# A four-layer decoder: VectorE and ScalarE in the order of the written table through the local transformer, the latent attention and the cross attention

## The chip, the core and the metric

The kernel runs on one core of a Trainium2 chip. Five engines work side by side: TensorE (PE, its weight loads shown as PEld), VectorE (DVE), ScalarE (ACT), GpSimd (POOL), and SyncE (SP), which issues transfers. Each engine takes its own instructions in a fixed order and waits at each for what it needs. The metric is the device time of one execution in microseconds; a profiled execution gives the trace that the views below come from.

## The reference

The program is a decoder of four layers on 32 sequences of 64 tokens with 128 features (2048 tokens). Each of its twelve stages is added to its input and put through a layernorm, `x = layernorm(x + stage(x))`:

- layer 0: self-attention with 16 heads of 8, a gated cross attention, and a *local transformer*;
- layer 1: a latent attention (16 heads of 64), a cross attention (16 heads of 8), and a mixture of 8 experts;
- layer 2: attention, cross attention and a second mixture of experts;
- layer 3: attention, cross attention and an fp8 linear layer.

The change touches mostly the local transformer, the latent attention and the first of layer 1's cross attentions. The local transformer is itself two layers deep. One of its layers, with 8 heads of 64 in which a query looks at its own sequence causally, is

```
qkv = shift(x) @ wqkv                 # half of the features from the token before
q, k = l2norm(q), l2norm(k); q, k = rotary(q, k)
x = x + softmax(q k^T) v @ wo
h = layernorm(shift(x)) * g + b
a, g = split(h @ w1 + b1)
x = x + (a * gelu(g)) @ w2 + b2
```

The latent attention projects queries directly and keys and values through a latent vector of 64, rotates queries and keys, and has no feed-forward part.

## The kernel before

All tensors stay on chip between stages. Tokens are kept in 4 blocks of 512 (NBLK), each as 4 tiles of 128 tokens (TPB), on one side with tokens on partitions (`xt`), on the other transposed (`xT`).

**The table.** Work is written as small functions that are put into a table under a step and a place in that step, `sp.at(step, place, f)`; `Steps.run` calls them in sorted order. TensorE always takes its instructions in that order. VectorE and ScalarE do so only in steps that lie in one of the ranges of `sp.fixed`, which are (95, 129) and (136, 197) before the change. Elsewhere a planner orders them, and it orders GpSimd and SyncE everywhere, from its own estimates of durations and with the table's order as priority. All waits between engines follow from the data.

**Steps.** The first attention begins at step 0, the gated cross attention at 14, the local transformer at 23 (16 tiles for each of its two layers), the latent attention at 55 (16 tiles), the cross attention `l1x` at 71 (16 score steps), then routing and experts, and from 96 on layer 2.

**One tile.** `tiles64` spreads a tile i over five steps. With "lag" counted from the step of i: `start` (lag 0, place 1) projects queries, keys and values into PSUM (`qkps`, `v`); in the local transformer ScalarE squares `qkps` (`sq`, line 1125) and copies `v`, VectorE sums the squares per head (`rn`, 1129), GpSimd raises them to the power -1/2 (1130 and the next line). `rope` (lag 0, 2.3) makes three VectorE products with the cosine and sine tables (`turn`), which GpSimd adds and multiplies by `rn`. `rotate` (lag 2, place 0) transposes the result on TensorE (`ropeT`, 969) and ScalarE copies it (`qk`, 970). `score` (lag 2, place 2) multiplies queries with keys into `s`; VectorE takes the maxima (`mx`, 988) and subtracts them (`p`), and ScalarE takes the exponential at once (992). `normal` (lag 2, 2.6) sums `p`, takes the reciprocal and multiplies: on VectorE with 8 heads (the local transformer, `nh == 4`), with the product on GpSimd with 16. `probs` (lag 3, place 4) transposes `p` (`ptps`, copied as `pT`, 1011), `values` (lag 3, place 6) multiplies with the values (`o`, copied as `oT`, 1027), `out` (lag 4, place 5) applies `wo` and, every second tile, adds to the residual on VectorE (`x` in the local transformer, `z` in the latent attention).

So step n holds rotate(n-2), start(n), score(n-2), rope(n), normal(n-2), probs(n-3), out(n-4), values(n-3), n being the tile's number.

**The feed-forward part**, once per block of four tiles, is placed around these. With n the block's first step: `shifted` (n-1, place 7) makes the shifted input `hT` with two ScalarE copies and one GpSimd memset (1103 to 1106); `normed` (n+7, 7) shifts the attention's result with a matmul (`shps`), copies it to `xs` on ScalarE, takes its statistics on VectorE and the inverse deviation on GpSimd (`rstd`), and scales on VectorE (1173); `turn_h` (n+8, 7) transposes `xs` (`hnT`); `hidden` (n+9, 7) multiplies with w1 in three chunks (`gps`, `aps`), gelu on ScalarE, product on VectorE (`ge`); `second` (n+10, 3) adds the bias row and residual on GpSimd (`resid`), multiplies with w2, adds on VectorE (`acc`), and in the second layer computes and applies the stage's layernorm (`norm`: statistics on VectorE, `rstd` on GpSimd, `nb` on VectorE, four scalings `x` on ScalarE). The latent attention calls `norm` in the same way from `done`, at a block's last tile, and `turn_x` transposes the result two steps later.

**PSUM.** Two buffers "S" of 1024 columns are shared by `qkps` and `s`, four buffers "G" of 512 columns by everything else; a matmul waits until its buffer's last reader is done.

**attn8 and routing.** In `l1x` the exponential stands at place 0.01 of its score's step; in attentions that are `held` or `ahead` at 6.5. With `split`, the last block is finished in two halves: `turn` and `normal_rest` of the second half stand at places 6.5 and 6.4 of step base+17 in the cross attentions `l1x` and `l2x` (the last one, `l3x`, has places of its own). Routing (`routed`) works in five pieces of 4, 4, 4, 2 and 2 tiles of tokens: logits, compare, choose, chosen, rows, then per tile `places` and `scatter`, one indirect transfer in GpSimd's queue each. In step `ready`+9 stand the third piece (places 1.1 to 4.4), the fourth (4 to 6.3) and the fifth (7 to 7.5); after them come the expert tables with the loads of the sorted rows through SyncE's queue (`tables`, in layer 2 `loads`).

Of the kernel before, what the change touches and what calls it, by code (L numbers as in the profile page):

```python
# [16 lines left out]
AF = mybir.ActivationFunctionType  # L17
# [264 lines left out]
class Decoder:  # L282
# [392 lines left out]
    def attn8(self, sp, base, name, src=None, rope=None, scale=1.0, row=None, mask=(None, None), has_out=True, split=False, number=False, turned=None, ahead=None, held=False):  # L675
# [142 lines left out]
        for blk in range(NBLK):  # L818
            for i in range(3):
                n = base + 4 * blk - 4  # L820
                at = (n + 1 + (i + 1) // 2, 4 + i % 2 / 2) if held and blk else (n + i, 4)
                sp.at(*at, lambda blk=blk, i=i: prepare(blk, i))
            sp.at(base + 4 * blk + (1 if split and not has_out else 2), 5.5, lambda blk=blk: resid(blk))
            if halved(blk):
                sp.at(*((base + 16, 6.5) if turned is None else (base + 16, 5.8)), lambda blk=blk: turn(blk, (0, 2)))
                sp.at(*((base + 17, 6.5) if turned is None else (base + 17, 2.1)), lambda blk=blk: turn(blk, (2, 2)))
                sp.at(*((base + 16, 6.4) if turned is None else (base + 16, 5.3)), lambda: normal_rest(0))
                sp.at(*((base + 17, 6.4) if turned is None else (base + 17, 2)), lambda: normal_rest(1))
            else:
                at = (base + 4 * blk + 8, 6) if has_out or blk < NBLK - 2 else (base + 16, 4.1)  # L830
                sp.at(*at, lambda blk=blk: turn(blk, (0, TPB)))
        if split and not has_out:
            sp.at(base + 15, 0.4, last_rest)
        for n in range(4 * NBLK):
            sp.at(base + n, 0, lambda n=n: score(n))
            sp.at(base + n, 6.5 if held or ahead else 0.01, lambda n=n: exps(n))
            end = split and n == 4 * NBLK - 1
            sp.at(*((base + n + 1, 4) if end else (base + n + 2, 2)), lambda n=n: turn_p(n))
            sp.at(*((base + n + 1, 6.1 if has_out else 5.6) if end else (base + n + 2, 5)), lambda n=n: values(n))
# [132 lines left out]
    def scores64(self, qT, kT, nh):  # L972
# [17 lines left out]
        self.tt(pr.rearrange("p n u k -> p u n k"), s4, bc(mx, 3, S), ALU.subtract)  # L990
        p3 = pr.rearrange("p n u k -> p (n u) k")
        nc.scalar.activation(p3, p3, AF.Exp)
        return p3

# [36 lines left out]
    def tiles64(self, sp, first, n, project, twist, turn, nh, wo, done):  # L1031
# [15 lines left out]
        def score(i):  # L1047
            (q, k), v = st[i]
            st[i] = (self.scores64(q, k, nh), v)

        def normal(i):
            self.normal64(st[i][0], nh)
# [20 lines left out]
        for i in range(n):  # L1073
            for lag, place, f in (
                (2, 0, rotate), (0, 1, start), (2, 2, score), (0, 2.3, rope), (2, 2.6, normal), (3, 4, probs), (4, 5, out),
                (3, 6, values),
            ):
                sp.at(first + i + lag, place, lambda f=f, i=i: f(i))


    def local_transformer(self, sp, base, names):

        nc = self.nc
        cur, tabs = {}, []

# [26 lines left out]
        def project(i):  # L1112
# [13 lines left out]
            v = self.q2([P, 2, 4, 64], "v64")  # L1126
            nc.scalar.copy(v, vp)
            rn = self.sb([P, 16], "rn", 3)
            nc.vector.tensor_reduce(rn, sq, AX.X, ALU.add)  # L1129
            nc.gpsimd.tensor_scalar(rn, rn, 1e-24, None, ALU.max)  # L1130
            self.tt(rn, rn, self.nhalf[:, 0:16], ALU.pow, nc.gpsimd)
            return (ps, rn), (v[:, 0], v[:, 1])

        def twist(i, t):
            ps, rn = t
            tab = tabs[i // 16]
            full = lambda a: a.unsqueeze(2).to_broadcast([P, 2, 8, 64])
            t1 = self.rope64(ps, full(tab[:, :, 0, :]), full(tab[:, :, 1, :]))
            self.tt(t1, t1, bc(rn, 2, 64), ALU.mult, nc.gpsimd)
            return t1  # L1140
# [18 lines left out]
        def normed(l, blk):  # L1159
# [8 lines left out]
            for t in range(TPB):  # L1168
                nc.vector.bn_stats(st[:, t, :], xs[:, t, :])
                nc.vector.bn_aggr(mv[:, t, :], st[:, t, :])  # L1170
            r = self.rstd(mv[:, :, 1], TPB)
            for t in range(TPB):
# [15 lines left out]
        def hidden(l, blk):  # L1188
# [10 lines left out]
            ff[l, blk] = hs  # L1199

        def second(l, blk):
            w, hs = self.w[names[l]], ff.pop((l, blk))
            x1 = x1s.pop((l, blk))
            xb = self.residual(x1, self.rows[f"l0f_b2{l}"])
            if l:
                self.tt(xb, xb, cur[0, blk], ALU.add, nc.gpsimd)
# [12 lines left out]
        self.tiles64(sp, base, 32, project, twist, turn, 4, lambda i: self.w[names[i // 16]]["wo"], done)  # L1219
        for l in range(2):  # L1220
            for blk in range(NBLK):
                n = base + 16 * l + 4 * blk
                for lag, place, f in ((-1, 7, shifted), (7, 7, normed), (8, 7, turn_h), (9, 7, hidden), (10, 3, second)):
                    sp.at(n + lag, place, lambda f=f, l=l, blk=blk: f(l, blk))
                if l:
                    sp.at(n + 12, 3, lambda blk=blk: self.turn_x(blk))


    def latent_attn(self, sp, base, name):

        nc = self.nc
        tab = self.c["r1"].rearrange("p (c s d) -> p c s d", c=2, d=64)
        lats, zs = {}, {}

# [43 lines left out]
        def done(i, y):  # L1278
# [100 lines left out]
    def routed(self, sp, st, ready, wr, br, base, rows, dst, bound, gated):  # L1379
# [29 lines left out]
        def scatter(t0, t):  # L1409
# [29 lines left out]
    def sorted_experts(self, sp, name, ready, fetched, tiles, back):  # L1439
# [136 lines left out]
        sp.at(*fetched, fetch)  # L1576
        sp.at(ready + 9, 8.1, tables)
        for j, at in enumerate(tiles):
# [12 lines left out]
    def capacity_experts(self, sp, name, ready, fetched, tiles, back):  # L1591
# [275 lines left out]
def decoder_kernel(ctx: ExitStack, tc: tile.TileContext, ins, at, out):  # L1867
# [76 lines left out]
```

## Time and profile before

| | |
|---|---|
| runs, median of 3 | 1419.74 us (1419.65 to 1423.8) |
| the profiled execution | 1420.89 us, its span 1419.1 us |
| mean granted TensorE clock | 0.912 |
| busy, PE / DVE / ACT / POOL | 1214.1 / 934.2 / 687.9 / 742.1 us |
| from step 29's first projection to the last score of `l1x` | 212.24 to 865.73 us of the span |
| the last score of `l1x` to the first sorted rows on TensorE | 865.73 to 900.28 us, PE busy 18.35 us |

A row of the timeline has the start, the length, the engine, line and operation, what it writes and reads, and in brackets the engine's idle time before it with what ended that. In a view by windows each row has the window, its length, the busy time of PE, PEld, DVE, ACT and POOL with counts, the granted clock (1 is full), the DMA share and GB/s. A view of waits lists who waited for whom: total, times, longest. Many operations share a helper's line (343 for matmuls, 346 for elementwise operations of two tensors), so they are told apart by tile names.

### The profile page before, as it was taken

The page shows a single profiled execution, that of the slowest core. Times are in us where ns is not written, and L with a number is a line of the kernel's source. Part 1 is how long each engine was busy: PE and PEld are TensorE (multiplying, and loading weights), DVE is VectorE, ACT ScalarE, POOL GpSimd, SP SyncE. Part 2 cuts the span into 40 slices and gives each one's busy share as a digit, 9 for nine tenths or more (in the row PEclk, how much of TensorE's full clock was granted, in tenths as well). Part 3 has the DMA queues.
Part 4 walks back from the last instruction along what each step waited for, and adds up shares of the span by engine and source line. Part 5 has one row for each costly group of instructions (what it writes and reads, how often), then busy time and mean ns, then how long its engine had stood idle before and what let it go on. Part 6 is the DMA issues. An engine that isn't in the chain of part 4 may idle for free.

```text
span 1419.1 us, 37013 instructions
## 1 busy us (share of the span) xinstructions
PE 1214.1 (86%) x16009; PEld 881.2 (62%) x16009; DVE 934.2 (66%) x1856; ACT 687.9 (48%) x1172; POOL 742.1 (52%) x618
## 2 busy tenths in 40 slices
PE   7998888899888978998898998697999948889991
PEld 4775455566555555666567776594678747567771
DVE  6754667778876766756575575554668743756797
ACT  2453445555555444544455553363556524344552
POOL 3533688767876664544464244352355443336553
PEclk9999889999999989999999997697999968879995
DMA  6001010080010000010001100220001101000001
GB/s 239 3 2 26 1 46 1 28 271 2 1 55 1 1 1 1 2 68 2 2 2 35 36 2 28 70 78 23 9 3 48 37 8 29 9 9 3 2 2 30
DMA packets 33715, 43.16 MB, mean 30 GB/s; under 512 B 5946, under 2 KB 27121, under 8 KB 33168
## 3 DMA queue, kind: packets, MB, share of 16 engines
q1 hardware_dynamic: 31536, 38.20, 8.4%
q8 instruction: 126, 2.06, 0.6%
q0 software_dynamic: 2016, 2.60, 0.6%
q14 instruction: 37, 0.30, 0.1%
HBM read 26.63 MB, written 15.56 MB: 30 GB/s over the span
## 4 chain that ended last, share of the span: by engine, by line
PE 49%; DVE 20%; POOL 14%; ACT 8%; issue 6%; DMA 2%; POOLq 0%; SPq 0%; DVEq 0%; ACTq 0%
PE s L343 10%; PE o L343 9%; DVE turn L346 5%; POOL turn L346 5%; PE qkps L343 5%; PE ptps L669 5%; PE proj L343 4%; PE y L343 3%; PE ropeT L969 3%; DVE p L346 2%; ACT pT L671 2%; DVE rn L1129 2%; POOL token_y L1362 2%; POOL rn L346 2%; POOL rstd L346 2%
## 5 line engine op out<-in xcount | busy, mean ns | idle before, releaser
L346 POOL TENSOR_TENSOR turn<-turn,turn 128x1024 f32<-128x1024 f32 x64 | 150.8, 2364 | 97.0 <-DVE turn L346 96.5
L656 DVE TENSOR_REDUCE mx<-s 128x16 f32<-128x1024 f32 x96 | 117.3, 1222 | 115.4 <-PE s L343 108.6
L346 DVE TENSOR_TENSOR p<-s,mx 128x1024 f32<-128x1024 f32 (+1 forms) x144 | 158.9, 1103 | 6.0
L671 ACT COPY pT<-ptps 128x512 f32<-128x512 f32 x192 | 103.9, 588 | 81.0 <-PE ptps L669 79.1
L726 ACT ACTIVATE p<-p 128x1024 f32<-128x1024 f32 x96 | 101.3, 1056 | 49.9 <-DVE p L346 49.7
L343 PE MATMUL s<-kx,q 32*64 32x128 f32 x3072 | 111.3, 283 | 6.0 <-DVE q L346 2.7
L346 DVE TENSOR_TENSOR turn<-qkps,w_const 128x512 f32<-128x512 f32 (+1 forms) x96 | 75.9, 858 | 58.6 <-PE qkps L343 58.6
L440 POOL TENSOR_SCALAR rstd<-bnmv 128x4 f32<-128x4 f32 (+1 forms) x60 | 16.6, 276 | 181.9 <-DVE bnmv L489 157.0
L343 PEld LDWEIGHTS s<-kx,q 32*64 32x64 f32 x3072 | 87.1, 137 | 37.9 <-issue 30.9
L669 PE MATMUL ptps<-w_const,p 128*128 128x128 f32 x768 | 109.4, 288 | 0.7 <-ACT p L726 0.5
L669 PEld LDWEIGHTS ptps<-w_const,p 128*128 128x128 f32 x768 | 90.4, 148 | 10.1 <-issue 8.5
L346 POOL TENSOR_TENSOR rn<-rn,nhalf 128x16 f32<-128x16 f32 x32 | 93.8, 2932 | 2.7
L343 PEld LDWEIGHTS o<-v,pT 128*64 128x64 f32 x2176 | 73.5, 141 | 33.8 <-ACT pT L671 16.5
L594 POOL TENSOR_TENSOR kx<-k,w_const 128x1024 f32<-128x1024 f32 x31 | 59.2, 1929 | 65.2 <-ACT k L603 31.1
L969 PE MATMUL ropeT<-w_const,turn 128*128 128x128 f32 x512 | 71.1, 286 | 24.7 <-ACT oT L1027 11.0
L343 PE MATMUL o<-v,pT 128*64 128x18 f32 x2176 | 82.2, 215 | 6.4 <-ACT pT L671 4.7
L969 PEld LDWEIGHTS ropeT<-w_const,turn 128*128 128x128 f32 x512 | 59.5, 146 | 36.3 <-ACT oT L1027 10.2
L346 DVE TENSOR_TENSOR turn<-qkps,xtab 128x512 f32<-128x512 f32 (+1 forms) x96 | 81.9, 857 | 0.0
L1129 DVE TENSOR_REDUCE rn<-sq 128x16 f32<-128x1024 f32 x32 | 39.0, 1217 | 62.6 <-ACT sq L1125 62.6
L343 PE MATMUL o<-pT,v 64*64 64x64 f32 x2048 | 72.3, 224 | 8.9 <-ACT pT L1011 8.9
L509 POOL TENSOR_SCALAR x<-z,bnmv,rstd 128x128 f32<-128x128 f32 x98 | 78.1, 810 | 2.6
L343 PE MATMUL qkps<-wbig,hT 128*128 128x512 f32 x128 | 71.0, 683 | 9.7 <-POOL hT L1105 8.8
(345 smaller groups left out, 2811.3 us busy)
## 6 DMA issues: line engine op xcount, KB each, us to landing
sorted_x<-zero SPq DMA_DIRECT2D x9, 990.0 KB
wbig<-in_l1f_w_dram SPq DMA_DIRECT2D x4, 1156.0 KB
wbig<-in_l2f_w_dram SPq DMA_DIRECT2D x16, 256.0 KB
wbig<-in_l0f_dram SPq DMA_DIRECT2D x2, 1561.0 KB
z<-token_y SPq DMA_DIRECT2D x8, 256.0 KB
wbig<-in_l1a_dram SPq DMA_DIRECT2D x1, 1856.0 KB
xsorted<-sorted_x SPq DMA_DIRECT2D x23, 66.0 KB
xT<-in_xT_dram SPq DMA_DIRECT2D x4, 256.0 KB
```

Of the source, the lines that this page charges most:

```text
L343: self.nc.tensor.matmul(out, lhsT=lhsT, rhs=rhs, start=start, stop=stop)
L346: (eng or self.nc.vector).tensor_tensor(out=out, in0=a, in1=b, op=op)
L440: nc.gpsimd.tensor_scalar(r[:, :n], var, EPS, None, ALU.add)
L509: eng.tensor_scalar(x[:, t0 + t, :], z[:, t0 + t, :], mv[:, t, 0:1], r[:, t : t + 1], ALU.subtract, ALU.mult)
L594: self.wide = eng.tensor_tensor(out=kx, in0=bc(kT, 1, 2), in1=bc(head[:, 2 * i : 2 * i + 2], 2, TB), op=ALU.mult).ins
L656: nc.vector.tensor_reduce(mx, s3, AX.X, ALU.max)
L669: self.nc.tensor.transpose(ps[:, j, :], flat[:, c : c + P], self.ident)
L671: self.nc.scalar.copy(o, ps)
L726: nc.scalar.activation(prs[n], prs[n], AF.Exp)
L969: self.nc.tensor.transpose(pt[:, j * P : (j + 1) * P], f[:, j * P : (j + 1) * P], self.ident)
L1129: nc.vector.tensor_reduce(rn, sq, AX.X, ALU.add)
L1362: i = self.nc.gpsimd.indirect_dma_start(dst, bass.IndirectOffsetOnAxis(at, 0), src, None, bounds_check=bound, oob_is_err=False).ins
```

## The change

VectorE and ScalarE are put in the table's order in the steps 29 to 88 as well (`sp.fixed.append((29, n + 18))`, where n is 71), and the range that ended before step 129 now ends before 130. In these steps places are changed:

- `tiles64`: `exps` becomes a function of its own at lag 2, place 6.5; `normal` moves to lag 3, place 0.5 (8 heads) or lag 2, place 6.6 (16 heads); `rope` moves from 2.3 to 1.5. In the transformer the sums of squares and their power (`rn`) move from `project` behind the three products in `twist`.
- Feed-forward: `shifted` to (n-1, 3.5); `normed` to (n+8, 1.7), with its scaling split off as `centred` at (n+9, 0.6); `turn_h` to (n+9, 3.5); the sum of residual, bias row and (second layer) the layer's input split off from `second` as `biased` at (n+7, 7), three steps ahead, on GpSimd.
- The closing layernorms of transformer and latent attention are split: statistics where they were, the scaling as `ended` at place 6.6 of the same step.
- `attn8`: the exponential at 6.5 everywhere but in the first attention; the second half's `normal_rest` and `turn` at 4.06 and 4.07 in `l1x` and `l2x`.
- Routing: the fourth piece from 6 to 6.3 up to 4.6 to 4.9, the fifth piece's logits from 7 to 4.5; `tables` and `loads` to the next step.

```diff
-                sp.at(*((base + 17, 6.5) if turned is None else (base + 17, 2.1)), lambda blk=blk: turn(blk, (2, 2)))
+                sp.at(*((base + 17, 4.07) if turned is None else (base + 17, 2.1)), lambda blk=blk: turn(blk, (2, 2)))
...
-                sp.at(*((base + 17, 6.4) if turned is None else (base + 17, 2)), lambda: normal_rest(1))
+                sp.at(*((base + 17, 4.06) if turned is None else (base + 17, 2)), lambda: normal_rest(1))
...
-            sp.at(base + n, 6.5 if held or ahead else 0.01, lambda n=n: exps(n))
+            sp.at(base + n, 6.5 if base else 0.01, lambda n=n: exps(n))
...
-        nc.scalar.activation(p3, p3, AF.Exp)
-        return p3
+        return pr.rearrange("p n u k -> p (n u) k")
...
+        def exps(i):
+            nc = self.nc
+            nc.scalar.activation(st[i][0], st[i][0], AF.Exp)
...
-                (2, 0, rotate), (0, 1, start), (2, 2, score), (0, 2.3, rope), (2, 2.6, normal), (3, 4, probs), (4, 5, out),
-                (3, 6, values),
+                (2, 0, rotate), ((3, 0.5) if nh == 4 else (2, 6.6)) + (normal,), (0, 1, start), (0, 1.5, rope), (2, 2, score), (3, 4, probs), (4, 5, out),
+                (3, 6, values), (2, 6.5, exps),
...
-            rn = self.sb([P, 16], "rn", 3)
-            nc.vector.tensor_reduce(rn, sq, AX.X, ALU.add)
-            nc.gpsimd.tensor_scalar(rn, rn, 1e-24, None, ALU.max)
-            self.tt(rn, rn, self.nhalf[:, 0:16], ALU.pow, nc.gpsimd)
-            return (ps, rn), (v[:, 0], v[:, 1])
+            return (ps, sq), (v[:, 0], v[:, 1])
...
+            t1 = self.rope64(ps, full(tab[:, :, 0, :]), full(tab[:, :, 1, :]))
+            rn = self.sb([P, 16], "rn", 3)
+            nc.vector.tensor_reduce(rn, sq, AX.X, ALU.add)
             nc.gpsimd.tensor_scalar(rn, rn, 1e-24, None, ALU.max)
             self.tt(rn, rn, self.nhalf[:, 0:16], ALU.pow, nc.gpsimd)
             self.tt(t1, t1, bc(rn, 2, 64), ALU.mult, nc.gpsimd)
...
+        def biased(l, blk):
+            xb = biases[blk] = self.residual(x1s[l, blk], self.rows[f"l0f_b2{l}"])
+            if l:
+                self.tt(xb, xb, cur[0, blk], ALU.add, nc.gpsimd)
...
-                self.norm(blk, x2, pool=False)
+                ends[blk] = x2, self.moments(blk, x2)
+        def ended(blk):
+            x2, moments = ends.pop(blk)
+            self.normed(blk, x2, moments, False)
...
-                for lag, place, f in ((-1, 7, shifted), (7, 7, normed), (8, 7, turn_h), (9, 7, hidden), (10, 3, second)):
+                for lag, place, f in (
+                    (-1, 3.5, shifted), (7, 7, biased), (8, 1.7, normed), (9, 0.6, centred), (9, 3.5, turn_h), (9, 7, hidden), (10, 3, second),
+                ):
...
+                    sp.at(n + 10, 6.6, lambda blk=blk: ended(blk))
...
-                self.norm(blk, zs.pop(blk), pool=False)
+                ends[blk] = self.moments(blk, zs[blk])
...
+            sp.at(base + 4 * blk + 7, 6.6, lambda blk=blk: ended(blk))
...
-            (12, 2, [(n + 9, 4)], (n + 9, 4.05), (n + 9, 6), (n + 9, 6.1), (n + 9, 6.2), [(n + 9, 6.3)] * 2),
-            (14, 2, [(n + 9, 7)], (n + 9, 7.1), (n + 9, 7.2), (n + 9, 7.3), (n + 9, 7.4), [(n + 9, 7.5)] * 2),
+            (12, 2, [(n + 9, 4)], (n + 9, 4.05), (n + 9, 4.6), (n + 9, 4.7), (n + 9, 4.8), [(n + 9, 4.9)] * 2),
+            (14, 2, [(n + 9, 4.5)], (n + 9, 4.51), (n + 9, 7.2), (n + 9, 7.3), (n + 9, 7.4), [(n + 9, 7.5)] * 2),
...
-        sp.at(ready + 9, 8.1, tables)
+        sp.at(ready + 10, 0, tables)
...
-        sp.at(ready + 9, 8.1, loads)
+        sp.at(ready + 10, 0, loads)
...
+    sp.fixed.append((29, n + 18))
...
-    sp.fixed.append((n - 1, n + 33))
+    sp.fixed.append((n - 1, n + 34))
```

More of the change, by code (lines that the diff above doesn't have):

```diff
@@ L990, in scores64 @@
         self.tt(pr.rearrange("p n u k -> p u n k"), s4, bc(mx, 3, S), ALU.subtract)
-        p3 = pr.rearrange("p n u k -> p (n u) k")
-        nc.scalar.activation(p3, p3, AF.Exp)
-        return p3
+        return pr.rearrange("p n u k -> p (n u) k")
     def normal64(self, p3, nh):
@@ L1083, in local_transformer @@
         nc = self.nc
-        cur, tabs = {}, []
+        cur, tabs, ends, biases = {}, [], {}, {}
         def tables():
@@ L1127, in project, with twist @@
             nc.scalar.copy(v, vp)
+            return (ps, sq), (v[:, 0], v[:, 1])
+        def twist(i, t):
+            ps, sq = t
+            tab = tabs[i // 16]
+            full = lambda a: a.unsqueeze(2).to_broadcast([P, 2, 8, 64])
+            t1 = self.rope64(ps, full(tab[:, :, 0, :]), full(tab[:, :, 1, :]))
             rn = self.sb([P, 16], "rn", 3)
@@ L1131, in project @@
             self.tt(rn, rn, self.nhalf[:, 0:16], ALU.pow, nc.gpsimd)
-            return (ps, rn), (v[:, 0], v[:, 1])
[L1134 to L1138, printed above, removed]
             self.tt(t1, t1, bc(rn, 2, 64), ALU.mult, nc.gpsimd)
@@ L1169, in normed, with centred @@
                 nc.vector.bn_stats(st[:, t, :], xs[:, t, :])
+            for t in range(TPB):
                 nc.vector.bn_aggr(mv[:, t, :], st[:, t, :])
-            r = self.rstd(mv[:, :, 1], TPB)
+            ff[l, blk] = xs, mv, self.rstd(mv[:, :, 1], TPB)
+        def centred(l, blk):
+            xs, mv, r = ff[l, blk]
             for t in range(TPB):
@@ L1199, in hidden @@
             ff[l, blk] = hs
+        def biased(l, blk):
+            xb = biases[blk] = self.residual(x1s[l, blk], self.rows[f"l0f_b2{l}"])
+            if l:
+                self.tt(xb, xb, cur[0, blk], ALU.add, nc.gpsimd)
         def second(l, blk):
             w, hs = self.w[names[l]], ff.pop((l, blk))
[L1203 to L1206, printed above, removed]
+            x1s.pop((l, blk))
+            xb = biases.pop(blk)
             y = self.ps8("G", "y2")
@@ L1232, in latent_attn @@
         tab = self.c["r1"].rearrange("p (c s d) -> p c s d", c=2, d=64)
-        lats, zs = {}, {}
+        lats, zs, ends = {}, {}, {}
         def latent(blk):
@@ L1284, in done, with ended @@
             if t == TPB - 1:
-                self.norm(blk, zs.pop(blk), pool=False)
+                ends[blk] = self.moments(blk, zs[blk])
+        def ended(blk):
+            self.normed(blk, zs.pop(blk), ends.pop(blk), False)
         self.tiles64(sp, base, 16, project, lambda i, t: t, turn, 8, lambda i: self.w[name]["wo"], done)
```

## The prediction

> **What bounds the kernel now.** First the page's head: span, busy shares, chain that ended last.
>
> ```profile
> span 1419.1 us, 37013 instructions
> PE 1214.1 (86%) x16009; PEld 881.2 (62%) x16009; DVE 934.2 (66%) x1856; ACT 687.9 (48%) x1172; POOL 742.1 (52%) x618
> ...
> PE 49%; DVE 20%; POOL 14%; ACT 8%; issue 6%; DMA 2%; POOLq 0%; SPq 0%; DVEq 0%; ACTq 0%
> ```
>
> TensorE is busy 86% of the time and half the chain, so a gain can only come out of TensorE's idle time (and of a lower clock after it). So I cut the changed stretch into blocks of four steps of the local transformer (window, length, busy PE, PEld, DVE, ACT, POOL, granted clock):
>
> ```profile
> 348.54:392.63 44.09, 39.22 (x441) 26.09 (x439) 34.60 (x55) 24.41 (x39) 33.34 (x20) 1.00 0.01 1
> 392.63:436.72 44.09, 39.22 (x440) 26.08 (x439) 34.61 (x55) 24.42 (x39) 33.35 (x20) 1.00 0.13 45
> 436.72:489.46 52.74, 43.02 (x444) 28.42 (x443) 36.88 (x64) 26.31 (x44) 36.01 (x23) 0.94 0.01 1
> 489.46:545.57 56.11, 46.73 (x459) 31.46 (x457) 37.48 (x68) 25.87 (x45) 29.81 (x18) 0.91 0.01 1
> ```
>
> A quiet block idles 4.87 us; the two in which the second layer's closing layernorm falls idle 9.7 and 9.4 us and run slower. From step 29 (212.24 us) to the last scores of the cross attention (865.73) these are TensorE's waits, the largest first:
>
> ```profile
> PE s L343 <- ACT qk L970: 11.3, 3, 4.0
> PE ropeT L969 <- ACT oT L1027: 11.0, 7, 2.5
> PE s L343 <- DVE turn L346: 10.1, 16, 2.5
> PE shps L343 <- DVE x L346: 9.4, 6, 1.8
> PE ropeT L969 <- ACT lat L1239: 7.7, 2, 3.9
> PE o L343 <- ACT pT L1011: 7.0, 10, 2.2
> ```
>
> With the smaller ones some 70 us: the ceiling of a gain, and every wait is for VectorE or ScalarE. How the present order makes them is read in the timeline (start, length, engine, operation, idle before). A quiet step, then the layernorm's:
>
> ```profile
> 361.84 1.22 DVE L1129 TENSOR_REDUCE rn<-sq 128x16 f32<-128x1024 f32 x1 [1.82 <-ACT sq L1125]
> 362.98 1.21 DVE L346 TENSOR_TENSOR turn<-qkps,xtab 128x1024 f32<-128x1024 f32 x1
> 364.11 0.68 DVE L988 TENSOR_REDUCE mx<-s 128x8 f32<-128x512 f32 x1
> 364.71 0.68 DVE L346 TENSOR_TENSOR turn<-qkps,xtab 128x512 f32<-128x512 f32 x1
> 366.50 0.41 DVE L346 TENSOR_TENSOR x<-y,x 128x256 f32<-128x256 f32 x1
> 366.66 2.37 POOL L346 TENSOR_TENSOR turn<-turn,turn 128x1024 f32<-128x1024 f32 x1 [0.24 <-ACT p L992]
> 366.97 0.70 PE L343 MATMUL shps<-x,w_const 128*128 128x256 f32 x2 [1.70 <-DVE x L346]
> ```
> ```profile
> 452.76 0.16 DVE L522 SCALAR_TENSOR_TENSOR nb<-bnmv,rstd 128x4 f32<-128x4 f32 x1 [1.25 <-POOL rstd L346]
> 452.96 1.65 ACT L515 ACTIVATE x<-acc,nb,rstd 128x128 f32<-128x128 f32 x4 [6.09 <-DVE nb L522]
> 454.51 1.04 ACT L970 COPY qk<-ropeT 128x512 f32<-128x512 f32 x2
> 455.61 0.69 PE L343 MATMUL s<-qk,qk 64*64 64x64 f32 x32 [4.00 <-ACT qk L970]
> ```
>
> VectorE waits 1.82 us for ScalarE's squares while the rotation's products, whose input is there, stand behind; the shift matmul stands in TensorE's queue 1.70 us before its input; and the layernorm's four scalings sit in ScalarE's queue, waiting for VectorE (6.09 us idle), ahead of the copies that the scores need.
>
> **The change, part by part.** No arithmetic is added or removed: the same instructions, in an order written out for VectorE and ScalarE, with TensorE's order edited.
>
> *Shift matmul* from (7,7) to (8,1.7): it comes after the next step's projections, about 3 us of matmuls later (qkps 1.9, v 1.1), so its 1.70 us wait goes once per block. Its statistics now stand on VectorE between the row sums of squares and the scores' maxima: four bn_stats and four aggregates, 1.4 us (369.50 to 370.8 before).
>
> *hT* from (-1,7) to (-1,3.5): the waits of qkps for it (0.47 in quiet blocks, 3.06 and 1.97 at two places) go; its two copies (0.6 each) now stand ahead of pT in ScalarE, which delays "o" some 0.5 once per block.
>
> *Products before row sums of squares* (rn): VectorE starts at qkps' end. The power on GpSimd (2.93) then runs after its add (2.36), not before: from the row sums' end 0.25 + 2.93 + 2.2, ready about 10.5 us after qkps' end, as now (360.7 to 371.3); TensorE takes it two steps on, at least 15 us. Hidden by that margin; without it 1 to 2 us a tile.
>
> *Softmax sums a step later, exponentials at 6.5.* Here the change adds a wait. The exponential stands behind oT, the last copy of a step; behind it in ScalarE stand the layernorm's scalings and the next step's qk copies, for which the scores wait. VectorE then has one closed loop per step: sum, reciprocal, product 0.65 + 0.2 + 1.65 (the product's mean of 29 is 1650 ns), rotation 2.4, row sums 1.2, maxima 0.6, subtraction 0.65, then out to ScalarE and back 0.9 (exponential 0.63 and two hand-overs): 8.25 us. TensorE needs 7.4 in a bare step (qkps to the end of o 358.87 to 365.27, ropeT 1.0). The step with the statistics needs 9.65 against 7.9. So VectorE falls about 2.6 us behind in two steps and catches up under hidden (5.8 us of matmuls) and second (2.8). Laid out over four steps, TensorE waits for the centred rows at hnT about 1.7, for qk 0.5, for pT 0.5, and 1.1 in crumbs (ropeT behind a late GpSimd, gps behind the gelu): 3.8 in place of 4.87.
>
> *Table loads.* Each block keeps two switches between exponential and gelu, but one now lies between oT and the exponential at the end of second's step, on VectorE's loop. The row: the load at 343.85 took 1.28 and the gelu began at 345.14, nothing in between. The Trainium skill (ScalarE: Activation LUTs, What ACT_TABLE_LOAD costs) counts a drain of about 1.38 with it, 2.66 in all; by that eight blocks would lose up to 11 us more. I take the row, and leave the 11 to the range.
>
> *biased* three steps ahead: 1.1 (layer two 2.4) of GpSimd leaves the wait of acc (0.93 on VectorE); it can delay one GpSimd product.
>
> *Closing layernorm a step behind* (ended at 6.6). In the transformer nb no longer blocks: statistics after second, 1.3 us of GpSimd, then nb at the step's end. The scalings (1.65) now come after the exponential, and delay qk: the scores wait about 1.9 instead of 4.0, and the waits that followed (1.80, 1.97) fall away. In the latent attention the same order gives reduction and nb about 3.5 us after o ends, scalings to 5.3, lat copy to 5.8, while TensorE stands from 2.5: 3.3 instead of 3.8.
>
> *Clock.* After the 4.00 us gap the block's matmuls ran slower (y 1.92 against 1.06): busy 43.02 against 39.22. The skill (TensorE: Matmul & The Clock Gate, Part 1) puts the drop at an idle window of about 3.4 us. By that the latent's 3.3 would keep the clock, worth some 2 us each; but here the 3.06 us gap at 281.52 was already followed by qkps at 3.00 for 1.88. I take the row: the clock returns in the transformer's two blocks (1.9), not in the latent.
>
> *Cross attention and routing.* TensorE waits there only a few us (93.67 busy of 101.48), so 0. In the tail the last half block's transpose and logits come earlier (logits of tiles 14 and 15 about 2 us here, 4 us after the second cross attention), but the end is set by GpSimd's queue: eight scatters about 1.27 us apart from 886.36 to 896.75, started by the third piece, whose place is kept. Moving the fourth piece's scatters ahead and the tables to a later step lets nothing start earlier: -1 for both tails, between -3 and +3.
>
> **Sum.** Quiet blocks from 212 to 437 (five): 1.1 x 5 plus half of the two odd hT waits, -8. The two layernorm blocks: each would save 2 + 1.8 + 2 in waits and about 3 in clock less what new waits take, 5 of 7 to 9 taken, -10. Transformer's last two blocks, which overlap the latent, and the latent's three: -4. Tails -1. Together -23 on the profiled execution's 1420.89 (span 1419.1): 1398. The runs' median is 1.15 lower: **1397**.
>
> **Rivals.**
> - *A, as summed* (0.52): 1397, own range 1383 to 1411.
> - *B, larger gain* (0.16): VectorE's loop hides fully under hidden and second, and quiet blocks fall to busy time plus 1 (40.2): 3.9 x 5 + 9 x 2 + 7: about 45, 1375. For it: VectorE is busy 34.6 of 44; against: the loop of 8.25 over 7.4.
> - *C, new waits for old* (0.10): the block stays at 44; the layernorm's gain is spent on the latent. 1419, within 0.3%.
> - *D, slower* (0.22): the strict loop. VectorE's 34.6 a block plus the return trip decides when a trip costs over 2.3 us (34.6 + 4 x 2.3 + 0.3 = 44.1): with GpSimd late or the exponential behind a table load it may be 3, 46.9 a block; over 7.5 blocks +21: 1440. For it: every wait here is a hand-over, and now nothing passes a late one.
>
> **How the numbers follow.** 0.3% (4 us) is what a measurement can tell. Faster: A and B, 0.68; same: C, 0.10; slower: D, 0.22. Range: from B's 1375 less 3 to most of D's lower half, 1372 to 1434, which leaves out about 2 in 10.
>
> **What would show it.** Right: the wait of shps for x gone; a quiet block near 43 us with a wait of hnT for xs; the 4.00 us waits of s for qk at about 2; the granted clock of the layernorm blocks near 1; the tails within 1 us. Wrong: p L992 (exponential) waits that grow past 2 us, ropeT waiting for GpSimd's turn, or ScalarE's qk late in every step.

## The result and the profile after

The changed kernel takes 1465.87 us (median of 4 runs, 1462.41 to 1472.56) against 1420.57 for the kernel before in the same comparison: 1.032 times the time, 95% interval 1.029 to 1.035. The forecast was 1397. The head of the page of the changed kernel:

```profile
span 1464.2 us, 37029 instructions
PE 1226.4 (84%) x16009; PEld 884.4 (60%) x16009; DVE 906.4 (62%) x1856; ACT 684.5 (47%) x1172; POOL 734.5 (50%) x618
...
PE 53%; DVE 16%; POOL 15%; ACT 8%; issue 4%; DMA 2%; SPq 1%; POOLq 0%; DVEq 0%; ACTq 0%
```

VectorE, ScalarE and GpSimd all have less to do than before (DVE 906.4 for 934.2), and TensorE, with the same 16009 matmuls, is busy 12.3 us longer: its clock was lower (mean 0.902 for 0.912). So the 45.1 us that the span grew are 32.8 us more idle time of TensorE and 12.3 us of slower matmuls. By windows, cut at the same steps as before (window, length, busy PE, PEld, DVE, ACT, POOL, granted clock, DMA):

```profile
373.21:425.21 52.00, 42.30 (x440) 27.03 (x439) 31.28 (x55) 24.33 (x39) 32.12 (x20) 0.93 0.00 1
...
477.22:533.99 56.77, 44.46 (x445) 29.07 (x443) 32.27 (x64) 26.37 (x44) 34.70 (x23) 0.91 0.00 1
533.99:585.94 51.95, 44.62 (x459) 29.45 (x458) 35.74 (x70) 25.35 (x45) 29.36 (x18) 0.93 0.01 1
```

A quiet block of four steps grew from 44.09 to 52.00 us: idle from 4.87 to 9.70, busy from 39.22 to 42.30 at a clock of 0.93 instead of 1.00, although VectorE is busy 31.3 us in it and was busy 34.6. Where the 45.1 us lie, against the terms of the sum:

| stretch | predicted | measured |
|---|---|---|
| up to step 29 | 0 | +4.0 |
| five quiet blocks | -8 | +36.5 |
| the two blocks with the closing layernorm | -10 | -0.1 (+4.0, -4.2) |
| rest of the transformer, latent attention | -4 | +3.7 |
| `l1x` to its last score | 0 | +1.2 |
| its tail; everything behind it | -1 | +3.4; -3.5 |

TensorE's waits in that stretch (who, for whom, total, times, longest), with four of the largest:

```profile
PE qkps L343 <- POOL hT L1107: 26.2, 6, 4.6
PE hnT L1189 <- DVE xs L1179: 16.5, 6, 3.4
PE ropeT L969 <- ACT qk L970: 12.1, 8, 3.6
PE s L343 <- ACT qk L970: 10.9, 3, 4.2
```

The first was 5.9 us before, the second was not in that list, and each comes once in six blocks. The first names GpSimd, in an instruction that clears 64 by 8 numbers. In the timeline (start, length, engine, operation, idle before):

```profile
389.40 2.36 POOL L346 TENSOR_TENSOR turn<-turn,turn 128x1024 f32<-128x1024 f32 x1 [3.09 <-DVE turn L346]
391.72 0.26 POOL L1139 TENSOR_SCALAR rn<-rn 128x16 f32<-128x16 f32 x1
392.06 2.93 POOL L346 TENSOR_TENSOR rn<-rn,nhalf 128x16 f32<-128x16 f32 x1
395.07 1.90 POOL L346 TENSOR_TENSOR turn<-turn,rn 128x1024 f32<-128x1024 f32 x1
397.03 0.11 POOL L1107 MEMSET hT<- 64x8 f32 x1
397.19 3.78 PE L343 MATMUL qkps<-wbig,hT 128*128 128x512 f32 x4 [4.44 <-POOL hT L1107]
```

Sum, maximum, power, product: GpSimd runs the four without a break, and the memset of 0.11 us behind them. It reads nothing. TensorE stands for 4.44 us, and then takes 3.78 us for projections that take 1.88 at full clock. The next step's chain has the inverse deviation of the layernorm in the same place:

```profile
406.36 0.36 DVE L1173 BATCH_NORM_AGGREGATE bnmv<-bnst 128x2 f32<-128x6 f32 x4
410.29 1.90 POOL L346 TENSOR_TENSOR turn<-turn,rn 128x1024 f32<-128x1024 f32 x1
412.27 0.23 POOL L440 TENSOR_SCALAR rstd<-bnmv 128x4 f32<-128x4 f32 x1
412.59 1.04 POOL L346 TENSOR_TENSOR rstd<-rstd,nhalf 128x4 f32<-128x4 f32 x1
413.66 1.12 DVE L1179 TENSOR_SCALAR xs<-xs,bnmv,rstd 128x128 f32<-128x128 f32 x4 [3.29 <-POOL rstd L346]
414.15 1.01 PE L1189 MATMUL hnT<-w_const,xs 128*128 128x128 f32 x4 [2.63 <-DVE xs L1179]
```

The statistics are done at 406.72 (`bnmv`, the first row); `rstd` starts 5.55 us later, when the product is off GpSimd. VectorE, in the table's order, waits for it and lets nothing pass. The closing layernorm, which the change was to take out of the way of the scores, shows the same chain (its statistics were done at 486.85), and the scores wait 4.22 us where it was 4.00:

```profile
490.42 0.23 POOL L440 TENSOR_SCALAR rstd<-bnmv 128x4 f32<-128x4 f32 x1
490.73 1.04 POOL L346 TENSOR_TENSOR rstd<-rstd,nhalf 128x4 f32<-128x4 f32 x1
491.80 0.16 DVE L522 SCALAR_TENSOR_TENSOR nb<-bnmv,rstd 128x4 f32<-128x4 f32 x1 [4.96 <-POOL rstd L346]
492.00 1.65 ACT L515 ACTIVATE x<-acc,nb,rstd 128x128 f32<-128x128 f32 x4 [3.08 <-DVE nb L522]
493.56 1.04 ACT L970 COPY qk<-ropeT 128x512 f32<-128x512 f32 x2
494.65 1.10 PE L343 MATMUL s<-qk,qk 64*64 64x64 f32 x32 [4.22 <-ACT qk L970]
```

### The profile page after: what moved, and what is told of

The parts are those of the page before. It is cut to its first block, busy times and chain, and to the rows that moved or that the text cites. A ratio compares the mean times of both kernels' runs of the same rounds, so it can differ in the third digit from the quotient of the medians.

```text
span 1464.2 us, 37029 instructions
## 1 busy us (share of the span) xinstructions
PE 1226.4 (84%) x16009; PEld 884.4 (60%) x16009; DVE 906.4 (62%) x1856; ACT 684.5 (47%) x1172; POOL 734.5 (50%) x618
## 4 chain that ended last, share of the span: by engine, by line
PE 53%; DVE 16%; POOL 15%; ACT 8%; issue 4%; DMA 2%; SPq 1%; POOLq 0%; DVEq 0%; ACTq 0%
PE s L343 11%; PE o L343 9%; POOL turn L346 6%; PE y L343 5%; DVE turn L346 5%; PE qkps L343 5%; PE ptps L669 5%; PE proj L343 5%; POOL rn L346 4%; ACT pT L671 2%; PE ropeT L969 2%; PE ptps L1007 2%; PE aps L343 1%; PE gps L343 1%; DVE p L346 1%
## 5 line engine op out<-in xcount | busy, mean ns | idle before, releaser
L346 DVE TENSOR_TENSOR turn<-qkps,xtab 128x512 f32<-128x512 f32 (+1 forms) x96 | 77.5, 861 | 79.6 <-ACT sq L1127 79.6
L343 PE MATMUL qkps<-wbig,hT 128*128 128x512 f32 x128 | 77.6, 738 | 29.7 <-POOL hT L1107 29.7
L996 DVE TENSOR_REDUCE rec<-p 128x8 f32<-128x512 f32 (+1 forms) x48 | 41.4, 862 | 77.6 <-ACT p L1051 77.6
L1025 ACT COPY oT<-o 128x512 f32<-128x512 f32 x64 | 37.5, 585 | 84.5 <-PE o L343 84.5
```

The lines of the kernel that those rows point to most:

```text
L343: self.nc.tensor.matmul(out, lhsT=lhsT, rhs=rhs, start=start, stop=stop)
L346: (eng or self.nc.vector).tensor_tensor(out=out, in0=a, in1=b, op=op)
L996: nc.vector.tensor_reduce(sm, p3, AX.X, ALU.add)
L1025: self.nc.scalar.copy(oT, ops)
```

## The experiments

Two theories. **Q**, GpSimd's queue: the new places put small operations that others need at once (memset, `rstd`) behind the step's contiguous chain of sum, power and product on GpSimd. **L**, the loop of rival D: VectorE and ScalarE in a strict order can't let anything pass a late operation. The experiments ran on chips on which the kernel before took 1404 to 1421 us, so all results are given as ratios to it, with 95% intervals. Where an expectation is in us, it is meant for a kernel before of 1420.57 us, and the text below it gives it as a ratio too. Edits are to the changed kernel, unless said otherwise.

**1. The memset on VectorE.**

```diff
-            nc.gpsimd.memset(h3[:, :, 0:1], 0.0)
+            nc.vector.memset(h3[:, :, 0:1], 0.0)
```

> Changed kernel, with one instruction on another engine: the memset of hT (0.11 us, once per block) on VectorE in place of GpSimd. Theory Q (GpSimd's queue: short instructions that TensorE waits for stand behind the tile's power and products): the six waits of qkps for hT (26.2 us in all) and the slow matmuls after each (qkps 3.78 for 1.88, v 1.89 for 1.08, 2.7 a time) go, about -40: 1425, between 1418 and 1436. Theory L (the strict loop of VectorE and ScalarE sets the pace, rival D of the prediction): TensorE then waits for VectorE instead, at most -12: 1454 or more.

1.0095 (1.0070 to 1.0119), inside Q's range (0.998 to 1.011) and far from L's (1.024 or more): one word takes away two thirds of the loss. The waits of qkps for hT are gone, and a quiet block takes 45.8 to 46.4 us. What is left is the second wait, which grew from 16.5 to 23.3 us, probably because TensorE now comes to it sooner:

```profile
338.91 0.23 POOL L440 TENSOR_SCALAR rstd<-bnmv 128x4 f32<-128x4 f32 x1
339.23 1.04 POOL L346 TENSOR_TENSOR rstd<-rstd,nhalf 128x4 f32<-128x4 f32 x1
340.30 1.11 DVE L1179 TENSOR_SCALAR xs<-xs,bnmv,rstd 128x128 f32<-128x128 f32 x4 [3.36 <-POOL rstd L346]
340.79 1.15 PE L1189 MATMUL hnT<-w_const,xs 128*128 128x128 f32 x4 [3.50 <-DVE xs L1179]
```

**2. The row sums ahead of the products again.**

```diff
             nc.scalar.copy(v, vp)
-            return (ps, sq), (v[:, 0], v[:, 1])
+            rn = self.sb([P, 16], "rn", 3)
+            nc.vector.tensor_reduce(rn, sq, AX.X, ALU.add)
...
+            return (ps, rn), (v[:, 0], v[:, 1])
```

> Changed kernel, with one part undone: the row sums of squares and their power (rn) ahead of the rotation's three products again. GpSimd's order, which follows from it, then has the memset of hT ahead of the tile's last product again. Theory Q: hT's wait falls from 4.4 to 0.5 to 1.5 and its slow matmuls go: 1430, between 1422 and 1442. Theory L: VectorE's loop keeps its length (the same instructions, one wait for the squares more): 1460 to 1472.

1.0088 (1.0068 to 1.0107), inside Q's range (1.001 to 1.015). The wait for hT fell to 1.20 us in five of the six blocks (3.22 in the first, 9.3 in all) with the memset left on GpSimd: the power now runs before the sum, as before the change, and the memset comes between sum (to 376.29) and product (from 376.54), no longer behind power and product. So two quite different edits shorten the same wait, and what they share is what stands ahead of the memset. The slow matmuls did not all go with it, as Q had expected (last section).

**3. The places without the order**, and **4. the order without the places** (the latter an edit to the kernel before).

```diff
-    sp.fixed.append((29, n + 18))
```

> Changed kernel without the fixed range of the steps 29 to 88: all places of the change, VectorE and ScalarE ordered by the planner there. Theory Q: the power still stands behind the add on GpSimd, so the memset is late in the same way: 1450 to 1468. Theory L: nothing is strict, so about the time before or better: 1405 to 1428.

```diff
     n = n + 48
+    sp.fixed.append((29, n + 18))
```

> Kernel before, with the fixed range of the steps 29 to 88 added and no place changed. Theory Q: rn stands before the products and shifted where it was, so GpSimd's order is as before; what is left is VectorE waiting for the squares and for the exponential in each step (about 1.1 and 0.9 us on 34.6 of 44 us a block, 42.6 a block): 1418 to 1436. Theory L: VectorE waits for the exponential inside the step, the loop is at its longest: above 1450.

Places alone: 1.0408 (1.0334 to 1.0482), no better than both together, and above Q's range too (1.021 to 1.033; L's was 0.989 to 1.005). The hT wait is 25.6 us, as in the changed kernel; so L is not what makes it. But the largest wait is one that neither theory had named, and that the changed kernel does not have:

```profile
PE v L343 <- ACT oT L1025: 39.1, 6, 7.2
```

The order alone: 1.1172 (1.1104 to 1.1240). That misses Q's range (0.998 to 1.011) and is on L's side (over 1.021), at a price nobody had put on it. On the old places the strict order is the loop of rival D; in the waits of that kernel (same columns as above):

```profile
PE o L343 <- ACT pT L1011: 85.6, 37, 10.5
PE shps L343 <- DVE x L346: 21.9, 7, 3.3
```

So L is a true mechanism, which the new places had already answered (in the changed kernel the waits of o for pT are 2.3 us): neither half of the change can be judged without the other.

**5. The layernorm's centring and turn later**, to give `rstd` time, with the memset on VectorE.

```diff
-                    (-1, 3.5, shifted), (7, 7, biased), (8, 1.7, normed), (9, 0.6, centred), (9, 3.5, turn_h), (9, 7, hidden), (10, 3, second),
+                    (-1, 3.5, shifted), (7, 7, biased), (8, 1.7, normed), (9, 2.5, centred), (9, 6.5, turn_h), (9, 7, hidden), (10, 3, second),
```

> The changed kernel with the clearing of hT's first column on VectorE, and the centring and the turn of the layernorm later in their step (places 2.5 and 6.5 instead of 0.6 and 3.5). Theory Q (GpSimd's row sums hold up the small operations behind them): what the first edit left is the wait of the hnT transposes for the centring, 23 us in six blocks, because the rstd stands behind the power and the product. A turn at 6.5 has some 5 us more, so that this wait falls from 3.9 to under 1.5 us a block, and the time to 0.998 of the kernel before (0.992 to 1.004). The rival M (the wait only moves on): the hidden products and the gelus behind them stand at place 7 of the same step and come as late as before; the wait shows at hidden or second instead, and the time stays at 1.006 to 1.012.

1.0162 (1.0134 to 1.0189): no gain, as the rival M had said, and worse than either number. VectorE no longer waits for `rstd` (done at 345.23), but now does the maxima and the subtraction first:

```profile
345.60 0.68 DVE L988 TENSOR_REDUCE mx<-s 128x8 f32<-128x512 f32 x1
346.31 0.69 DVE L346 TENSOR_TENSOR p<-s,mx 128x512 f32<-128x512 f32 x1
346.92 1.49 DVE L1179 TENSOR_SCALAR xs<-xs,bnmv,rstd 128x128 f32<-128x128 f32 x4
347.77 1.02 PE L1189 MATMUL hnT<-w_const,xs 128*128 128x128 f32 x4 [2.96 <-DVE xs L1179]
```

TensorE's transposes were moved with the centring, so that the wait stays (2.96 us a block) and the eviction of hnT, which lay beside other matmuls, now holds `gps` another 0.93. A wait is not cured by moving both its ends.

**6. The same with the row sums ahead of the products**, and **7. with the tally's copy on VectorE as well.**

> As the kernel with the later centring, and the row sums and the power are back in the step's projection, ahead of the rotation's products. Theory Q: the chain of row sums, power and product ends 1.2 us earlier on GpSimd, and what is left of hnT's and ropeT's waits shrinks: 0.990 of the kernel before (0.982 to 0.998). If the row sums' place is worth nothing once the clearing is off GpSimd, the time equals that of the kernel with the later centring within 0.3%.

```diff
-        self.nc.gpsimd.tensor_copy(before[:, 0, :], last)
+        self.nc.vector.tensor_copy(before[:, 0, :], last)
```

> As the last, and the copy of the tally's row (before) is on VectorE instead of GpSimd, in the two tails of the cross attentions. Theory Q: the products inc waited 3.40 us for that copy in the first tail, behind six scatters that GpSimd issues; without it the first tail is 2.5 to 3.5 us shorter and the second 0 to 3: 0.988 of the kernel before (0.980 to 0.996), 3 to 5 us under the last. The rival: the copy is read at once by products whose other operand is as late, and less than 1 us comes of it.

1.0199 (1.0170 to 1.0227) and 1.0210 (1.0180 to 1.0240): both far from Q's 0.990 and 0.988, and no faster than experiment 5. The trace of the first shows a price that nobody had counted. Its centring takes 4.75 us for the 1.12 of the changed kernel:

```profile
351.07 2.34 POOL L346 TENSOR_TENSOR turn<-turn,turn 128x1024 f32<-128x1024 f32 x1
351.24 4.75 DVE L1179 TENSOR_SCALAR xs<-xs,bnmv,rstd 128x128 f32<-128x128 f32 x4
353.49 1.90 POOL L346 TENSOR_TENSOR turn<-turn,rn 128x1024 f32<-128x1024 f32 x1
353.65 0.45 PE L1189 MATMUL hnT<-w_const,xs 128*128 128x128 f32 x1 [4.36 <-DVE xs L1179]
```

It lies beside the 4.3 us of GpSimd's two large operations, and ends 0.6 us after them; the first transpose, which needs only the first of its four instructions, starts 0.24 us after the sum's end. The later place and the reordered GpSimd brought the two together. In the second the 3.40 us wait of `inc` for the copy is gone, and the first tail (last score to first sorted rows on TensorE) is about 2 us shorter, 34.2 for 36.3, while the wait for the transfer of the sorted rows grew by 1.6 (6.8 to 8.4). In the runs' times none of it can be told apart (the intervals overlap), so what the copy is worth stays open; nothing in them speaks for the 3 to 5 us that were expected.

**8. The tails alone** (edit to the kernel before: the second half's `turn` and `normal_rest`, the fourth and fifth routing pieces, `tables`, `loads` and the range's end as in the change).

> The kernel before with the two tails of the change alone (pieces 12 and 14 of the routing, the turn of the second half, and tables and loads a step later, their order in the table's order); the local transformer untouched. From the two traces what follows the first cross attention's table became 3.5 us shorter, and that attention's tail 3.4 us longer: so a time equal to the kernel before's within 3 us, ratio 0.998 to 1.002, if the tails are independent of what stands before them. The prediction had put them at a gain of 1 us.

1.0000 (0.9981 to 1.0019), as expected.

**9. The statistics early.** After experiment 5, the wait had to be taken at its other end: `normed` ahead of the step's projection and rotation, the memset on VectorE.

```diff
-                    (-1, 3.5, shifted), (7, 7, biased), (8, 1.7, normed), (9, 0.6, centred), (9, 3.5, turn_h), (9, 7, hidden), (10, 3, second),
+                    (-1, 3.5, shifted), (7, 7, biased), (8, 0.9, normed), (9, 0.6, centred), (9, 3.5, turn_h), (9, 7, hidden), (10, 3, second),
```

> The changed kernel with the clearing of hT on VectorE, and the layernorm's shift product, copies, statistics and rstd at place 0.9 of their step instead of 1.7: ahead of the step's own projection, so ahead of its rotation on VectorE, where VectorE waits 1.8 us for the squares anyway. The rstd then stands ahead of the step's sum, row-sum power and product on GpSimd instead of behind them (some 5 us earlier). Theory Q: the wait of hnT for the centring, 3.50 us in each of six blocks with the clearing alone moved, goes, and the time from 1.0095 to 0.995 of the kernel before (0.989 to 1.001). The rival N (the change's later rotation products are what costs, whatever stands on GpSimd): the rstd's 1.3 us only push the row sums' power, and the rotation's transposes wait as much longer: 1.005 to 1.012.

0.9881 (0.9850 to 0.9912), faster than the kernel before and a little beyond Q's range. Windows, then the timeline:

```profile
319.71:361.49 41.78, 38.92 (x440) 26.14 (x438) 31.48 (x56) 24.14 (x39) 31.95 (x20) 1.00 0.01 2
```
```profile
324.53 0.23 POOL L440 TENSOR_SCALAR rstd<-bnmv 128x4 f32<-128x4 f32 x1
324.85 1.04 POOL L346 TENSOR_TENSOR rstd<-rstd,nhalf 128x4 f32<-128x4 f32 x1
325.86 2.37 POOL L346 TENSOR_TENSOR turn<-turn,turn 128x1024 f32<-128x1024 f32 x1
...
329.88 1.11 DVE L1179 TENSOR_SCALAR xs<-xs,bnmv,rstd 128x128 f32<-128x128 f32 x4
330.75 0.66 PE L1189 MATMUL hnT<-w_const,xs 128*128 128x128 f32 x4
```

`rstd` now stands ahead of the sum, 4.0 us before its reader; neither VectorE nor TensorE waits in this place, the clock is 1.00, and a quiet block takes 41.78 us: 10.2 less than with the change, 2.3 less than before it.

**10. With that, the row sums ahead of the products**, and **11. the early statistics alone**, the memset left on GpSimd.

> As the last, and the row sums and the power are back in the projection, ahead of the rotation's products. On GpSimd the power then stands ahead of the sum of the products. Theory Q: nothing late stands behind the row sums any more, so their place is worth little: equal to the last within 0.4%. If the later row sums still cost where the clearing and the rstd are clear of them, this one is 3 to 8 us faster than the last.

> The changed kernel with the layernorm's statistics at place 0.9 alone, the clearing of hT still on GpSimd. Theory Q: the waits of hnT (16.5 us) go, the waits of qkps for hT (26.2 us, 4.44 a block) stay as they are, since the rstd stands in another step than the clearing: 1.019 of the kernel before (1.013 to 1.026). If the two waits share one cause, so that one takes the other's place, the time stays at 1.030 or over.

0.9954 (0.9932 to 0.9977): slower than experiment 9 by 0.7%, so the equality that Q expected was missed, on the side that favours the change: products first is the better order once the small operations are out of the chain's way. The wait of hnT for xs is back there (15.9 us). The early statistics alone: 1.0194 (1.0147 to 1.0240) for an expected 1.019. The hT waits stay (23.1 us), the hnT waits go, so the two are separate. Taking away the first gave 2.2% and the second 1.3%; both together gave 4.4% (experiment 9), more than the sum. That fits experiment 1, where the second wait grew when the first was gone.

**12. The closing layernorms' scaling behind the next step's copies**, on top of experiment 9.

```diff
-                    sp.at(n + 10, 6.6, lambda blk=blk: ended(blk))
+                    sp.at(n + 11, 1.45, lambda blk=blk: ended(blk))
...
-            sp.at(base + 4 * blk + 7, 6.6, lambda blk=blk: ended(blk))
+            sp.at(base + 4 * blk + 8, 1.45, lambda blk=blk: ended(blk))
```

> As the kernel with the clearing on VectorE and the early statistics, and the closing layernorms (local and latent transformer) apply their scale another 0.4 to 0.5 of a step later: place 1.45 of the next step instead of 6.6 of their own, behind that step's copies of qk on ScalarE. Theory Q: the scores' wait of 4.22 us for qk (three times, 10.8 in all) and the latent's transposes' of 3.60 us (two) stand behind the normalization on ScalarE, which stands behind the rstd, which stands behind the row sums' power and the product on GpSimd: out of the table's order ahead of qk, the waits fall below 1 us each, 12 us in all, and the time to 0.981 of the kernel before (0.976 to 0.986). The rival: the wait is the copies' own (their ropeT is late) or moves to the transposes of the next cross attention: 0.986 to 0.992, equal to the kernel with the early statistics.

0.9803 (0.9767 to 0.9840) for an expected 0.981: 1378.78 us beside 1404.39 for the kernel before, the fastest of all. The copies go first, the scores have no wait, and the scaling follows:

```profile
438.02 1.05 ACT L970 COPY qk<-ropeT 128x512 f32<-128x512 f32 x2
438.96 1.04 ACT L1127 ACTIVATE sq<-qkps 128x1024 f32<-128x1024 f32 x1
439.55 0.69 PE L343 MATMUL s<-qk,qk 64*64 64x64 f32 x32
440.24 1.04 POOL L346 TENSOR_TENSOR rstd<-rstd,nhalf 128x4 f32<-128x4 f32 x1
441.31 0.16 DVE L522 SCALAR_TENSOR_TENSOR nb<-bnmv,rstd 128x4 f32<-128x4 f32 x1 [1.25 <-POOL rstd L346]
441.51 1.65 ACT L515 ACTIVATE x<-acc,nb,rstd 128x128 f32<-128x128 f32 x4 [1.05 <-DVE nb L522]
```

The latent's transposes still wait 2.07 us each (it had been 3.60), so that part of the expectation, under 1 us, was not met; and o now waits for pT behind the scaling (2.72 us at 444.88). Not tried: `hT` alone back at its old place, `rstd` on another engine, and GpSimd in the table's order.

## Why the prediction was wrong, and where it was right

**The step that failed is "Products before row sums of squares", in "Hidden by that margin".** Its arithmetic was fair: the chain on GpSimd ends 13.8 us after the projection's start (12.5 before), 1.4 us later than was figured, and its own reader two steps on doesn't miss it. But the margin was worked out for that reader alone. What else stands in GpSimd's queue was never asked: in the quiet blocks a memset (4.44 us a block) and `rstd` (2.63), and the slow clock behind the first (projections 3.78 for 1.88, in all 3.08 us more busy a block). New and grown waits, and the clock, less the waits that did go, make up the 7.9 us a block. Experiment 1 takes away the first (1.032 to 1.0095), experiment 11 the second (1.032 to 1.019), experiment 9 both (0.988). With both out of the way a quiet block idles 2.86 us, less than the 3.8 that were forecast: the rest of the block's account was not too hopeful.

The sign was there to be read. "Every wait is for VectorE or ScalarE" stops one line short in its own view of the kernel before, whose next line names GpSimd:

```profile
PE qkps L343 <- POOL hT L1105: 5.9, 3, 3.1
```

**hT.** "The waits of qkps for it go" counted two ScalarE copies and left out the third writer, the memset, although two of the waits that it named (3.06 and 1.97) were for the memset. One of these, at 466.21, also lies in a layernorm block and not in the quiet ones it was counted for. In a quiet block before the change the memset ran between sum and product, and the projection waited 0.47 us, for a copy:

```profile
369.09 0.11 POOL L1105 MEMSET hT<- 64x8 f32 x1
369.28 2.06 POOL L346 TENSOR_TENSOR turn<-turn,rn 128x1024 f32<-128x1024 f32 x1
```

Not its cost but its place was what mattered.

**Shift matmul.** The 1.70 us wait went, as said, and the statistics on VectorE, counted at 1.4 us, took 1.14. But place 1.7 is behind `rope` at 1.5, which put `rstd` behind the row sums' power and the product on GpSimd: 2.63 us at hnT in place of the predicted 1.7, which moreover was to come from VectorE's loop. At place 0.9 both waits are gone (experiment 9).

**Softmax a step later.** The loop of 8.25 us was mis-sized: the product that was put at 1.65 us took 0.69 (median of 28; in the kernel before most of them ran beside GpSimd's large operations, in the changed one mostly beside its power or while it stood idle), and VectorE's busy time a block fell by 3.3 us. VectorE doesn't start at qkps' end, though; it still waits for the squares (1.28 us). **Rival D** named the right sign by the wrong mechanism: the strict order is no loss on these places (1.032 with, 1.041 without) and a heavy one on the old (1.117).

**Closing layernorm.** "1.3 us of GpSimd, then nb" again took `rstd` as if it ran when its input was there; it took 1.3 us, and began when the product was off GpSimd (490.42; `nb` had stood 4.96 us). The scores waited 4.22, not 1.9. In the latent attention the wait for `lat` fell from 3.8 to 2.99 us, more than was forecast (3.3), but the scaling ahead of the copies of `qk` brought the transposes two new waits, 3.65 and 3.60. **Clock**: its return was drawn from the gain at the scores and did not come (granted clock 0.91 and 0.93 in the two blocks, before 0.94 and 0.91). Preferring the row to the 3.4 us of the Trainium skill (TensorE: Matmul & The Clock Gate, Part 1) was right: behind the two waits of 2.99 us for `lat` the projections took 3.15 and 3.62 us for 1.88.

**Right:** the table loads. They take 1.28 us, and the block with two of them runs in 41.78 us (experiment 9); the drain that the Trainium skill adds (ScalarE: Activation LUTs, What ACT_TABLE_LOAD costs) does not show there, since behind both loads the next activation starts within 0.02 us. The bias rows moved ahead cost nothing that shows. The tails, inside their range of -3 to +3: -0.2 with everything behind the first, and 1.0000 alone.

**Open:** the 4.0 us up to step 29. The transformer's first projection starts 0.8 us earlier than before (147.74 for 148.57), so they arise behind the gated cross attention, in steps 23 to 28, where the places are new and the planner still orders VectorE and ScalarE: 2.5 us of it are busy time at a lower clock (0.86 for 0.89). Which place costs it was not taken apart.

## What to carry to other kernels

When a change moves a long operation in an engine's queue, list everything that comes behind it in that queue, with its reader, and ask for each when it is needed: a memset of 0.11 us cost 4.44 us a block and the clock, and no row of busy time shows that. What cured a wait here was starting its producer earlier (experiment 9), or letting the waiting instruction stand behind others that are ready (12); moving the reader and all that hangs on it later did not (5). Orders written by hand come as a whole: the strict order alone was 12% slower, the places alone 4%, and both with three operations put right 2% faster than what they replaced.

## What the runs showed of the hardware

Some operations of VectorE slow down beside GpSimd's large ones. The centring of one block, four instructions on 128x128 float32, took 1.12 us in the changed kernel, 1.11 beside GpSimd's power on 128x16, and 4.75 beside its operations on 128x1024, while those kept their 2.34 and 1.90 us. The product of `p` takes 0.69 us beside the power (changed kernel, 393.36) and 1.87 beside the product on 128x1024 (experiment 6, 344.67). Others do not slow down: beside the sum at 389.40 the row sums took 1.21 us, the maxima 0.68 and the subtraction 0.69, as elsewhere. What sets them apart was not tested.

The clock does not follow the length of one gap. Behind 4.44 us qkps took 3.78 for 1.88; behind 3.65 (changed kernel, 602.43, at ropeT) the projection took its full-speed 1.88, and behind 2.99 (at ropeT, twice) 3.15 and 3.62. In experiment 2 the same wait of 1.20 us at hT was followed by 1.98 in one block (330.40) and by 3.51 in another (376.51). Behind 2.57 us (experiment 2, at hnT) y took 1.92 for 1.06; behind 2.63 (changed kernel, at hnT) and 2.72 (experiment 12, at o) y and qkps took their full-speed 1.06 and 1.88; behind 1.95 (experiment 12) ropeT took 1.67 for 1.09. What decides was not found.

The rotation's products do not read the squares, and still in no kernel here do they begin before ScalarE's squaring is over, also where they stand ahead of the row sums (1.28 us of idle time in the changed one). Both read the same buffer of PSUM; whether that is the reason was not tested.
